# A hybrid two-layer block on one core: score steps that wait for banks, a first group by sequences, ranks by kinds of steps

## The chip, the core and the metric

The kernel runs on one core of a Trainium2 chip. The metric is device time in microseconds (us) of one execution, lower is better; of the three timed runs of the kernel before, the median is taken. Five engines work side by side: PE (matrix multiplications and transposes), DVE (vector), ACT (activations), POOL (a slower vector engine) and SP (here only issuing DMAs). Each executes its own list of instructions strictly in order; they meet through semaphores. A "bank" is one of eight 128x512 f32 accumulators that PE writes and DVE or ACT read.

## What is computed

Eight sequences of 256 tokens with 128 features pass through eight residual layers. Cut to what matters:

```python
x = x + attn_a(ln(x))       # causal attention, one head
x = x + ffn_relu(ln(x))     # 128 -> 512 -> 128, then a layernorm of its own
x = x + attn_b(ln(x))       # linear attention (no softmax)
x = x + ffn_relu(ln(x))
x = x + retention(ln(x))    # 16 heads, causal with decay
x = x + ffn_silu(ln(x))     # 128 -> 384 -> 128
x = x + softmax_attn(ln(x)) # 16 heads of 8, not causal
x = x + ffn_silu(ln(x))
```

The softmax attention is the dearest layer. For each of 8 sequences and 16 heads it needs `softmax(q k^T / sqrt(8)) v` over 256 x 256 scores, with a contraction over 8 features.

## The kernel before, in words

**Tiling.** The eight sequences form four groups (GROUPS) of two. A group's activations `x[g]` lie in the on-chip memory as 128 partitions by 4 tiles (NT) of 128 features, from the first DMA to the last. Every layer of a group starts with `normalised` (L653): bn_stats for each tile on DVE (L577), then either the aggregation on DVE (L585) with four small operations on POOL (L592 to L597), or all of it on POOL in eight small operations (L601 to L608), then scale and shift on ACT (L614) or DVE (L619), then four transposes on PE (`transposed`, L635) and a copy from the bank (`copied`, L463).

**The order of the work is planned on the host.** The layers are Python generators that yield steps: an engine (or two, `either`) with an assumed duration. The class `Plan` runs all four groups as threads against a small model of the five engines: it repeatedly takes the engine that can start soonest, and of the steps that are able to start there the one with the lowest `turn`. `turn` is the thread's rank (table RANKS by group and layer) plus a nudge for some single steps by their number (NUDGES). On PE a step that has only just become ready gets LATE added, and one that would run into the refill of instructions (256 to a page, PAGE) gets STALL times the modelled pause. `either` compares two engines with a delay for the second: SPARE for copies, SHARED for the wide two-input additions and products of `wide_step` (L468), ROOT for the retention's square root, JOINED for the aggregation of a layernorm (0.55 us: the DVE is chosen when it could begin within that of POOL's choice). The emitted programs simply follow the resulting order, so all that a change of such numbers can do is to reorder instructions, and to move some from one engine to another.

**The softmax scores.** `pairs_of_scores` (from L1155) is one thread for all sequences. A "pair" is two heads. Scores are computed twice: first with queries on the partitions, from which DVE takes the row maxima (`maxima`, L1221, two reductions a pair), then, with the maxima folded in as a ninth feature, with keys on the partitions, from which ACT makes exponentials (`exponentials`, L1255, two activations a pair). Each pair fills two banks of a pool of its own, `score_bank`, which holds four banks, and six once the last group has come to this layer (`todo["alone"]`). A contraction over 9 rows uses one of four row tiles of PE, so two pairs of opposite parity can run at the same time, in one step of 8 matmuls (L1200) instead of two steps of 4. While `alone` is false a step with two pairs always waits for four banks. When it is true, it goes with two pairs only if more than one further bank is free already, otherwise with one pair, and the other goes back into the queue. `weighted` (L1272) then multiplies exponentials by values in column tiles, L1285 transposes, L1293 and L1294 divide by the sums, L1361 transposes again, and the output projection, the last FFN and the output DMA follow.

**The first group's first layer.** `causal_attention` (L672) normalises a group, multiplies it by two prepared matrices (`value` L675 by tiles, `queries` L688 on 512 columns at once), then treats its two sequences (scores L710, mask L715, maxima L719, exponentials L722, transposes L729, values L737 to L739, and DVE's addition into `x` at L746). Group 0 arrives in two DMAs, and its layernorm is done in two halves (`halved`), but the transposes of both halves stand together in one step. `keep_busy` (L428) issues ten matmuls whose results are not used.

Of the kernel before, what the change touches and what calls it, by code (L numbers as in the profile page):

```python
# [69 lines left out]
PAGE, PAGE_US = 256, 3.7  # L70


SPARE, AIDED, ROOT, SHARED, JOINED = 0, 5.07, 0.83, 0.1, 0.55
STALL = 1.59
LEEWAY = 0


RANKS = [
    [-2.06, -5.27, -3.76, -0.29, -1.05, -0.6, -7.92, 4.73],
    [-0.06, 1.15, 4.31, 3.86, 1.11, -5.08, 0.12, 3.75],  # L80
    [1.85, 2.45, 2.73, 4.11, 1.45, 1, 1.47, 4.34],
    [3.44, 5.35, 1.93, 5.94, 3.15, 2.72, -0.21, 3.88],
]

NUDGES = {
    3: 1.5, 276: 2.4, 353: 1.8, 375: 2.8, 404: -1.8, 482: -5, 489: -3.3, 562: -1.1, 607: 2.7,
    762: 5.1, 804: 2.5, 813: -6.6, 882: 6.4, 919: -0.7, 923: 6.5, 953: 0.8, 974: 2.7, 1000: -6,
    1280: -2.1, 1282: -3.3, 1329: 8.1, 1439: 1.9, 1447: 1.8, 1560: 4, 1673: 2.9, 1798: 3.6,
}
FIRST, LAST = -15.26, 8.75  # L90
LATE = 1.25


PORT_OF_DVE = "port of DVE"
# [5 lines left out]

def of_dve(n):
    return 0.066 + n / 960


class Thread:
# [42 lines left out]
class Plan:  # L148
# [4 lines left out]
    def __init__(self):  # L153
        self.free = {e: 0.0 for e in (PE, ACT, DVE, POOL, SP)}
        self.steps = {e: [] for e in self.free}
        self.stores, self.untils, self.sleeping = [], [], []
        self.table = None
        self.mode = None
        self.port = {DVE: 0.0, POOL: 0.0}
        self.page, self.used = -PAGE_US, 77  # L160
        self.current = None
        self.count = 0
        self.made = 0
        self.now = 0.0
# [25 lines left out]
    def resume(self, th, value):  # L190
        outer, self.current = self.current, th
        try:
            want = th.steps.send(value)
        except StopIteration as stop:
            th.done, th.result = True, stop.value
            for j in th.joiners:
                self.joined(j)
            self.current = outer
            return
        self.current = outer  # L200
        self.count += 1
        kind = want[0]
        if kind == "step":
            for e, us, table, delay in want[1]:
                at = th.after(e) + delay
                self.steps[e].append((at, th, self.count, us, table))
            th.mode, th.n = want[2:]
            self.made += 1
            th.turn = th.rank + NUDGES.get(self.made, 0.0)
        elif kind == "get":  # L210
            want[1].waiting.append((th, self.count, want[2]))
        elif kind == "join":
            th.join = want[1]
            for j in want[1]:
                j.joiners.append(th)
            self.joined(th)
        elif kind == "until":
            self.untils.append((th, want[1]))
        elif kind == "at":
            self.sleeping.append((want[1], self.count, th))  # L220
# [16 lines left out]
    def stall(self, th, start, us):  # L237
# [2 lines left out]
            return 0.0  # L240
        return max(0.0, self.page + PAGE_US - start - us * (PAGE - self.used) / th.n)

    def run(self):
        self.go = []
        while True:
# [11 lines left out]
                best = (min(self.sleeping)[0], None, None)  # L257
            for e, queue in self.steps.items():
                if queue:
                    start = max(self.free[e], min(self.ready(e, q) for q in queue))  # L260
                    if best is None or start < best[0]:
                        best = (start, e, None)
            for s in self.stores:
                found = s.next()
                if found and (best is None or found[0] < best[0]):
                    best = (found[0], None, s)
            if best is None:
# [9 lines left out]
            if s is not None:  # L277
# [6 lines left out]
                self.resume(w[0], got[0] if w[2] == 1 else got)  # L284
                continue
            able = [q for q in self.steps[e] if self.ready(e, q) <= start]

            late = {id(q): e == PE and q[0] > start - LOAD for q in able}
            extra = {
                id(q): LATE * late[id(q)] + (STALL * self.stall(q[1], start, q[3]) if e == PE else 0.0)  # L290
                for q in able
            }
            q = min(
                able, key=lambda q: (q[4] not in (None, self.table), q[1].turn + extra[id(q)], q[2])
            )
            _, th, _, us, table = q
            for queue in self.steps.values():
                queue[:] = [r for r in queue if r[1] is not th]
            if table not in (None, self.table):
                us += TABLE_LOAD  # L300
                self.table = table
# [47 lines left out]
def hybrid(ctx: ExitStack, tc: tile.TileContext, t: dict, out: bass.AP):  # L349
# [290 lines left out]
        put(bank, ps)  # L640
        return yT

    def halved(a, parts):
        n = a.shape[1] // parts
        return [a[:, k * n : (k + 1) * n] for k in range(parts)]

    def normalised(g, keep=False, tiles=slice(0, NT), quick=False):
        y = yield get(work)
        nt = tiles.stop - tiles.start
        y4 = view(y, "p (t d) -> p t d", nt * D, t=nt)  # L650
        parts = 2 if quick and g == 0 else 1
        yield join(
            [  # L653
                spawn(layernorm(a, b, quick))
                for a, b in zip(halved(x[g][:, tiles, :], parts), halved(y4, parts))
            ]
        )
        yT = yield from transposed(y4, 3 if parts == 2 else 0)
        if keep:
            return y, y4, yT  # L660
        put(work, y)
# [16 lines left out]


    def causal_attention(g):  # L680
        yT = yield from normalised(g, quick=True)
        yield until(lambda: "causal" in made)
        w = made["causal"]

        def queries():
            ps = yield get(bank)
            yield step(PE, 0.86, n=4)
            nc.tensor.matmul(ps, w[:, 0, :], yT[:, :N], start=True, stop=True)  # L688
            yield from copied(q[:, :N], ps, N)
            put(bank, ps)  # L690

        def value():
            ps = yield get(bank)
            yield step(PE, 0.89)
            by_tiles(ps, w[:, 1, :], yT)
            yield from copied(values[:, :N], ps, N)
            put(bank, ps)

        def sequence(b):
            at = b * S  # L700
            v = view(values, "p (t d) -> p t d", t=NT)
            blocks = ((0, 0, P), (P, P, 3 * P))
            p = yield get(work)
            pT = yield get(work)
# [37 lines left out]
            put(work, pT)  # L742
            yield step(DVE, 0.52)
            for i in range(2):
                xs = x[g][:, 2 * b + i, :]
                nc.vector.scalar_tensor_tensor(  # L746
                    xs, ps[:, i * P : (i + 1) * P], sums[:, i : i + 1], xs, ALU.mult, ALU.add
                )
# [4 lines left out]
        values = yield get(work)  # L753
        made_v = spawn(value())
        yield join([spawn(queries()), made_v])
        yield join([spawn(sequence(b)) for b in range(2)])
        put(work, yT, q, values)

    def linear_attention(g):
# [395 lines left out]
    def pairs_of_scores():  # L1155
# [7 lines left out]
        while todo["sequences"]:  # L1163
# [22 lines left out]
            else:  # L1186
                ps = yield get(score_bank, 2)
                if len(chosen) == 2:
                    if sum(i[0] <= plan.now for i in score_bank.items) > 1:
                        ps = ps + (yield get(score_bank, 2))  # L1190
                    else:
                        of_keys, *pair = chosen.pop()
# [203 lines left out]
    plan.start(causal_weights(), FIRST, 3.8)  # L1396
    for g in range(GROUPS):
        plan.start(layers(g), g, ARRIVALS[g])
    plan.start(constants(), LAST, 29.4)
    plan.start(linear_weights(), LAST, 20.2)  # L1400
    plan.start(retention_weights(), LAST, 29.7)
    plan.start(silu_weights(), LAST, 16.5)
    plan.start(softmax_weights(), LAST, 52.5)
    plan.start(pairs_of_scores(), FIRST, 0.0)
    plan.run()
    return plan
# [103 lines left out]
```

## Time and profile before

| what | value |
|---|---|
| median of three timed runs | 427.99 us |
| the three runs | 427.99, 432.9, 426.69 us |
| the profiled execution | 426.42 us |
| its span (first to last instruction) | 424.6 us |
| mean granted PE clock in it | 0.999 |
| busy, PE / DVE / ACT / POOL | 411.2 / 311.1 / 243.1 / 180.0 us |

In the profile, a row gives the kernel's line, the engine, the operation, the tiles written and read, and the number of instructions; then busy time, the mean of one, and the idle time of the engine before them. An f32 matmul stands as two MATMUL records, a transpose as one: a score step of one pair (4 matmuls) is 8 records, one of two pairs is 16. Starts of consecutive PE records are a better measure of what a step costs than its busy time, since neighbours overlap.

By time the kernel has three parts. Until 176 us the groups work through the causal, ReLU, linear and retention layers; from 177.2 us (the first L1200) to about 352 us softmax scores are mixed with all other layers; from there to 402 us the last sequences' scores are mixed with little else, and a last stretch of 18 us finishes them.

### The profile page before, as it was taken

Reading aid. Unit: us, or ns where it says so; the run is one execution under the profiler, and the core shown is the slowest. Engines: PE = TensorE matmul, PEld = TensorE weight load, DVE = VectorE, ACT = ScalarE, POOL = GpSimd, SP = SyncE. Lnnn points to the kernel's source line nnn. Section 1 sums busy time; section 2 is a strip of 40 time slices with the busy share of each in tenths; the row PEclk is TensorE's granted clock in tenths of the full one; section 3 lists DMA queues with packets and bytes.
Section 4 is the critical chain, followed back from the end, with each engine's and each line's share of the span. In section 5 each row is a group of like instructions: output and inputs, shape, how many; then the busy total and the mean of one; then the engine's idle time right before and its main releaser. Section 6 shows DMA issues by size and latency. Waiting matters only on the chain.

```text
span 424.6 us, 12624 instructions
## 1 busy us (share of the span) xinstructions
PE 411.2 (97%) x5136; PEld 293.4 (69%) x5136; DVE 311.1 (73%) x824; ACT 243.1 (57%) x499; POOL 180.0 (42%) x358
## 2 busy tenths in 40 slices
PE   6999899999999999999999999999999999999996
PEld 6776776974777676767766657667675766665576
DVE  6997867769898969689966889833797742993253
ACT  3678867439544335424665753658645676268741
POOL 4245666575867636314696422229240300110030
PEclk9999999999999999999999999999999999999999
DMA  7400000000203001520001140000100020100001
GB/s 244 176 1 2 1 2 0 2 0 17 37 15 41 3 4 24 60 22 4 4 6 27 28 50 5 4 21 12 28 2 13 3 53 15 29 2 2 2 14 37
DMA packets 8040, 10.72 MB, mean 25 GB/s; under 512 B 1000, under 2 KB 6888, under 8 KB 7984
## 3 DMA queue, kind: packets, MB, share of 16 engines
q1 hardware_dynamic: 7904, 9.81, 11.2%
q8 instruction: 40, 0.66, 0.7%
q14 instruction: 16, 0.13, 0.2%
q10 hardware_dynamic: 80, 0.13, 0.1%
HBM read 4.43 MB, written 1.05 MB: 13 GB/s over the span
## 4 chain that ended last, share of the span: by engine, by line
PE 83%; DVE 8%; POOL 4%; ACT 2%; issue 1%; DMA 1%; POOLq 0%; DVEq 0%
PE bank L1200 18%; PE bank L1272 7%; PE bank L1130 5%; PE bank L1120 5%; PE bank L1114 5%; PE bank L819 4%; PE bank L806 4%; PE bank L1012 4%; PE bank L940 3%; PE bank L675 3%; PE bank L635 2%; PE bank L973 2%; PE bank L1285 2%; PE bank L1314 2%; DVE work L474 2%; PE bank L997 1%
## 5 line engine op out<-in xcount | busy, mean ns | idle before, releaser
L1221 DVE TENSOR_REDUCE small<-bank 128x2 f32<-128x512 f32 x128 | 80.5, 681 | 21.5 <-PE bank L1200 21.1
L1255 ACT ACTIVATE probs<-bank 128x512 f32<-128x512 f32 x128 | 67.7, 601 | 40.7 <-PE bank L1200 40.5
L1200 PE MATMUL bank<-l_spread 32*128 32x256 f32 x1024 | 85.1, 400 | 0.0
L601 POOL TENSOR_SCALAR small<-small 128x16 f32<-128x16 f32 (+1 forms) x28 | 8.0, 287 | 160.2 <-DVE small L577 160.2
L1200 PEld LDWEIGHTS bank<-l_spread 32*128 32x128 f32 x1024 | 53.6, 184 | 22.4 <-issue 7.5
L463 ACT COPY work<-bank 128x512 f32<-128x512 f32 (+3 forms) x78 | 36.7, 488 | 53.9 <-PE bank L635 21.2
L614 ACT ACTIVATE work<-x,small 128x128 f32<-128x128 f32 x84 | 36.8, 487 | 29.3 <-POOL small L608 23.9
L463 DVE COPY work<-bank 128x512 f32<-128x512 f32 (+3 forms) x34 | 17.8, 537 | 26.9 <-PE bank L1272 14.9
L577 DVE BATCH_NORM_STATS2 small<-x 128x6 f32<-128x128 f32 x128 | 29.7, 278 | 6.9 <-DMA x<-in_x 3.7
L1272 PE MATMUL bank<-probs,l_values 128*32 128x256 f32 x512 | 33.3, 384 | 0.0
L1046 POOL TENSOR_TENSOR small<-small,mhalf 128x32 f32<-128x32 f32 x6 | 32.7, 5449 | 0.5
L806 PE MATMUL bank<-work,c_relu 128*128 128x512 f32 x64 | 30.5, 599 | 1.9 <-ACT work L463 0.9
L819 PE MATMUL bank<-c_relu,work 128*128 128x128 f32 x256 | 31.0, 276 | 0.0
L819 PEld LDWEIGHTS bank<-c_relu,work 128*128 128x128 f32 x256 | 29.8, 192 | 1.2 <-issue 1.1
L607 POOL TENSOR_TENSOR small<-small,mhalf 128x4 f32<-128x4 f32 (+1 forms) x28 | 27.9, 998 | 2.2
L670 DVE TENSOR_TENSOR x<-bank,x 128x256 f32<-128x256 f32 (+1 forms) x36 | 16.1, 450 | 15.1 <-PE bank L1130 9.1
L1114 PE MATMUL bank<-work,c_ints 128*128 128x256 f32 (+1 forms) x72 | 25.1, 462 | 0.3 <-DVE work L474 0.2
L1130 PE MATMUL bank<-c_ints,work 128*128 128x128 f32 x192 | 24.5, 278 | 0.0
L1130 PEld LDWEIGHTS bank<-c_ints,work 128*128 128x128 f32 x192 | 23.2, 192 | 1.9 <-issue 1.2
L1120 PE MATMUL bank<-work,c_ints 128*128 128x256 f32 (+1 forms) x72 | 24.4, 459 | 0.0
L1272 PEld LDWEIGHTS bank<-probs,l_values 128*32 128x32 f32 x512 | 14.1, 109 | 14.0 <-issue 5.1
L635 PE MATMUL bank<-ident,work 128*128 128x128 f32 x128 | 21.3, 283 | 1.2 <-ACT work L614 1.2
(172 smaller groups left out, 781.1 us busy)
## 6 DMA issues: line engine op xcount, KB each, us to landing
r_spread<-wide SPq DMA_DIRECT2D x32, 64.0 KB
l_spread<-wide SPq DMA_DIRECT2D x32, 64.0 KB
out<-x SPq DMA_DIRECT2D x8, 128.0 KB
x<-in_x SPq DMA_DIRECT2D x3, 256.0 KB
c_retention_vo<-in_retention_vo SPq DMA_DIRECT2D x1, 713.0 KB
c_relu<-in_relu SPq DMA_DIRECT2D x1, 706.0 KB
c_retention_qk<-in_retention_qk SPq DMA_DIRECT2D x1, 641.0 KB
c_ints<-in_ints SPq DMA_DIRECT2D x1, 576.0 KB
```

Of the source, the lines that this page charges most:

```text
L463: (nc.scalar.copy if e == ACT else nc.vector.tensor_copy)(dst, src)
L614: nc.scalar.activation(y[:, i, :], src[:, i, :], AF.Identity, bias=shift[:, i : i + 1], scale=rstd[:, i : i + 1],)
L806: nc.tensor.matmul(ps, w1[:, c * P : (c + 1) * P], yT[:, :N], start=True, stop=True)
L819: nc.tensor.matmul(ps[:, n * D : (n + 1) * D], h[c][:, i * P : (i + 1) * P], w2[:, c, :], start=(c == 0), stop=(c == 3),)
L1046: nc.gpsimd.tensor_tensor(root, var, minus_half, ALU.pow)
L1114: nc.tensor.matmul(ps[:, :n], w_gate[:, cols], yT[:, :n], start=True, stop=True)
L1120: nc.tensor.matmul(ps[:, :n], w_up[:, cols], yT[:, :n], start=True, stop=True)
L1130: nc.tensor.matmul(ps[:, (i - first) * D : (i - first + 1) * D], h[c][:, i * P : (i + 1) * P], w_down[:, c, :], start=(c == 0), stop=(c == 2),
L1200: nc.tensor.matmul(to[k][:, n * S : (n + 1) * S], seq.spread[rows, j, of_keys, n * P : (n + 1) * P], seq.spread[rows, j, 1 - of_keys, :], ...
L1221: nc.vector.tensor_reduce(nmax[:, h2 % 4 // 2, 2 * (h2 % 2) + k, :], ps[k].rearrange("p (m s) -> p m s", m=2), AX.X, ALU.max, negate=True,)
L1255: nc.scalar.activation(p[:, k, :], ps[k], AF.Exp)
L1272: nc.tensor.matmul(o[32 * i : 32 * (i + 1), (j % 2) * S : (j % 2 + 1) * S], seq.v[:, c, VONE * h : VONE * h + 32], seq.p[h2][0][:, k, c * ...
```

## The change

Numbers of the plan are replaced, three pieces of code are changed, and the rest is bookkeeping that only makes the planning quicker.

```diff
-SPARE, AIDED, ROOT, SHARED, JOINED = 0, 5.07, 0.83, 0.1, 0.55
-STALL = 1.59
-LEEWAY = 0
+SPARE, AIDED, ROOT, SHARED, JOINED = 0, 5.07, 0.83, 0.1, 0
+STALL = 3.4
+WAITING = 0.6
+LEEWAY = 0.01
...
+KINDS = {
+    "add_to": -0.25, "value": 2.35, "finished": -2.57, "weighted": 0.66, "spread_heads": -0.83,
+    "pairs_of_scores": 0.61, "projected": -4.42, "down": 0.08, "maxima": -0.29, "queries": 0.54,
+    "linear_attention": 1.08,
+}
...
-FIRST, LAST = -15.26, 8.75
-LATE = 1.25
+FIRST, LAST = -7.99, 12.38
+LATE = 0.75
...
-            th.turn = th.rank + NUDGES.get(self.made, 0.0)
+            th.turn = th.rank + KINDS.get(kind_of(th.steps), 0.0) + NUDGES.get(self.made, 0.0)
...
-                    if sum(i[0] <= plan.now for i in score_bank.items) > 1:
+                    if sum(i[0] <= plan.now + WAITING for i in score_bank.items) > 1:
                         ps = ps + (yield get(score_bank, 2))
...
     def causal_attention(g):
-        yT = yield from normalised(g, quick=True)
+
+        parts = 2 if g == 0 else 1
+        n = NT // parts
+        yield join([spawn(causal_part(g, slice(k * n, (k + 1) * n))) for k in range(parts)])
+
+    def causal_part(g, tiles):
+        nt = tiles.stop - tiles.start
+        n = nt * P
+        yT = yield from normalised(
+            g, tiles=tiles, quick=True, waiting=3 if g == 0 and tiles.start == 0 else 0
+        )
...
-            yield step(PE, 0.86, n=4)
-            nc.tensor.matmul(ps, w[:, 0, :], yT[:, :N], start=True, stop=True)
-            yield from copied(q[:, :N], ps, N)
+            yield step(PE, 0.215 * nt, n=4)
+            nc.tensor.matmul(ps[:, :n], w[:, 0, :], yT[:, :n], start=True, stop=True)
+            yield from copied(q[:, :n], ps[:, :n], n)
...
-        yield join([spawn(sequence(b)) for b in range(2)])
+        yield join([spawn(sequence(b)) for b in range(nt // 2)])
```

`WAITING`: in the `alone` phase a score step with two pairs chosen takes both if two further banks come free within 0.6 us of the plan's present, and waits for them. `KINDS`: a step's turn now also depends on the generator that yields it, whatever the group. `causal_part`: group 0's first layer is two threads, one a sequence, each with its own transposes, products and copies of half the width. RANKS and NUDGES are other tables of the same form, the starting times of the five threads that prepare weights move (linear weights from 20.2 to 10.6 us of the plan, SiLU weights from 16.5 to 33.6), and JOINED becomes 0.

## The prediction

> **What bounds the kernel now.** I read the page's busy shares first, then its slices, the table of three stretches, the list of PE's waits, and last the timeline of PE where scores stand alone.
>
> ```profile
> PE 411.2 (97%) x5136; PEld 293.4 (69%) x5136; DVE 311.1 (73%) x824; ACT 243.1 (57%) x499; POOL 180.0 (42%) x358
> ...
> PE   6999899999999999999999999999999999999996
> DVE  6997867769898969689966889833797742993253
> ...
> PE 83%; DVE 8%; POOL 4%; ACT 2%; issue 1%; DMA 1%; POOLq 0%; DVEq 0%
> ```
>
> PE is busy in every slice but the first and last, and the chain that ended last lies on it for 83%. So the time is PE's own work plus what interrupts it.
>
> ```profile
> 0.00:176.00 176.00, 166.64 (x1896) 126.11 (x1897) 143.79 (x457) 102.90 (x225) 101.33 (x209) 1.00 0.15 36
> 176.00:352.00 176.00, 175.98 (x2597) 120.84 (x2595) 129.63 (x283) 100.33 (x196) 70.50 (x118) 1.00 0.12 18
> 352.00:403.00 51.00, 50.60 (x514) 31.15 (x510) 27.71 (x58) 32.35 (x63) 4.10 (x16) 1.00 0.05 10
> ```
>
> Columns: stretch, length, busy PE, PEld, DVE, ACT, POOL. PE idles 9.4 us before 176 us, where DVE is busy 82%, 0.02 us in the middle, 0.4 us in the score stretch, where DVE and ACT have room.
>
> ```profile
> PE bank L428 <- DMA x<-in_x: 3.3, 1, 3.3
> PE bank L635 <- ACT work L614: 1.2, 3, 0.5
> PE bank L806 <- ACT work L463: 0.9, 2, 0.7
> PE bank L806 <- POOL small L593: 0.9, 1, 0.9
> PE bank L710 <- DVE work L463: 0.8, 1, 0.8
> PE bank L869 <- ACT work L463: 0.7, 1, 0.7
> ```
>
> These are PE's longest waits, in total us. After the first DMA all are short: PE reaches a transpose, or a product of it, before the layernorm or the copy is through. All waits of the list but the first come to about 6.5 us.
>
> ```profile
> 351.05 1.15 PE L1200 MATMUL bank<-l_spread 32*128 32x256 f32 x16
> 352.13 0.71 PE L675 MATMUL bank<-c_softmax,work 128*128 128x128 f32 x4
> 352.77 1.13 PE L1200 MATMUL bank<-l_spread 32*128 32x256 f32 x8
> 353.83 0.44 PE L1361 MATMUL bank<-ident,work 128*128 128x128 f32 x2
> ```
>
> From start to start a score step of two pairs costs 1.08 us (351.05 to 352.13) and a step of one pair 1.06 (352.77 to 353.83): a lone pair pays nearly the price of two.
>
> **The change part by part.** The sum is made against the profiled execution: 426.42 us, span 424.6. The runs shown are 426.69, 427.99 and 432.9; the high one stands alone, so I take the mean of the two others, 427.3, as what a typical run gives, and set my result 0.9 above a profiled one.
>
> *Score steps.* In the built order of the kernel before there are 74 score steps, 54 of two pairs and 20 of one; in the changed one 71, with 57 and 14. All lone steps come behind the first 46 in both, that is in the alone stretch. So 6 x 1.06 - 3 x 1.08 = 3.1 us of PE work goes. No other engine's work changes (128 reductions of 681 ns, 128 exponentials of 601 ns stay). The Trainium skill speaks against a part of it: "TensorE: Matmul & The Clock Gate", section "Measured speedup vs the span model", gives four row tiles 3.07 times the rate of one, not 4. If two tiles gave a full 2, a step of four tiles would take 2/3.07 x 2 = 1.30 times a step of two, and the saving would be 6 x 1.06 - 3 x 1.38 = 2.2 us. The rows above show 1.02 times. I take the trace's 3.1.
>
> The price is the wait. The step of two pairs now stands in PE's order where four banks are expected up to 0.6 us late; all of PE's stream queues behind it. The banks are freed by DVE (681 ns each) or ACT (601 ns each), so a late reduction delays weighted, transposes and FFN steps alike. Bounds: nothing, if other work in front covers it (DVE 54%, ACT 63% busy there), and 0.6 us for each of the 3 new double steps, 1.8 us. Nearest row: PE's 0.4 us idle in this stretch; I take 0.4 more.
>
> *Changes of mode.* Steps between plain matmuls and the tile modes follow each other 204 times instead of 197. In the timeline a plain 128x256 matmul hands on after 0.44 us to its like (340.27 to 340.71 us), and after 0.52 us to a score step (340.71 to 341.23), so 0.08 us each: +0.6 us.
>
> *Layernorms.* JOINED at 0 sends 34 of 40 aggregations to DVE, before 12. POOL's eight rows sum to 2.72 us for four tiles (299+206+203+221+230+287+1072+199 ns), its four remaining ones to 1.78 us, and four aggregations take 0.37 us on DVE: each of 22 chains gets 0.57 us shorter. This only pays where the transposes wait. The loads for L635 were held up by L614 15 times, 5.6 us in all; at 0.37 us each, about 10 such waits cut by 0.2 to 0.57 us give 2 to 5.6. I take -2.2. POOL's share of layernorms falls by about 20 us.
>
> *Steps between engines.* DVE gains 78 aggregations (44 took 4.2 us, so +7.4), three more copies of 128x512, four of 128x256 and two of 128x384 with two fewer small ones (+4.3), four scalings (+1.4), one root (+2.5), and gives up 8 wide additions to POOL (-5.5) and three bias steps (-2.2): about +8 us, mostly before 200 us. ACT loses about 3. This is covered only while DVE is not queued: at 82% it has 32 us free there, with the 8 us 86%.
>
> *Short cover.* The moves of RANKS, KINDS and NUDGES reorder nearly everything, so I compared the two built orders at one thing that durations can price: PE steps that need a copy of an earlier PE result. For 128x512 the copy (586 ns) and two hand-overs need about 0.94 us of other PE work in between. Before, 17 places have over 0.15 us too little, 8.8 us altogether, and the trace shows them (0.84 us at L869, 1.07 us at an L806). Changed, it is 21 places and 11.4 us, several in the first layers and three after the last scores. That is +2.6 us. I have no row for the order of the rest; by this measure it is not better.
>
> *Instruction refills.* STALL doubles. Score steps of the trace that exceed their 1.08 us with no wait (1.55, 1.46, 1.39 us and the like) lose about 1.8 us together; the bounds are -1.8 and, if heavy steps now crowd elsewhere, +1.8. I take -0.9.
>
> *First group.* Its products start with the first half. In the trace the transposes start at 7.87 us behind unused matmuls from 6.00 to 7.65, and ten of those stay; what can go are waits of 0.4 and 0.9 us behind transposes up to 17 us. But four copies at half width cost fixed parts, and the two orders have like short cover there. Bounds -1.3 and +0.5; I take -0.4.
>
> No DMA is added or dropped: SP issues the same 32 + 32 spreading DMAs and the same loads. Their places move; r_spread and l_spread land while PE has other layers to do, before 352 us. Weight preparation is moved by up to 17 us, but stays in front of its first user.
>
> Sum: -3.1 + 0.4 + 0.6 - 2.2 + 2.6 - 0.9 - 0.4 = -3.0 us; 426.42 - 3.0 = 423.4 profiled, 424.3 as a typical run.
>
> **The rivals.** *Fast: the new order removes the waits as well.* If all 6.5 us of the listed waits and the 1.8 us of refills went with the 3.1 us of score steps: 426.42 - 11.4 = 415.0, or 416 typical. For it: the shorter layernorm chains act exactly where PE idles, and PE's own work does not stop it: without these waits there is nothing else in the middle. Against it: the 21 short-cover places.
>
> *Slow: DVE becomes the bound before 200 us.* The eight wide additions moved to POOL cost 1.27 us each there instead of 0.68, so POOL has 34 instead of 26. The Trainium skill, "SBUF — State Buffer", section "Summary: rules for kernel authors", says that when DVE has two inputs in that memory and POOL reads it too, the second to issue is blocked until the first is done. The trace shows such a case: a POOL operation L606 of 0.20 us took 0.77 us beside a DVE addition of 0.67. By the rows alone DVE's demand there is 144 + 8 = 152 of 176 us; by the rule in full, the 10.2 us of added POOL time block DVE too, and it is 162, 92%. From about that share on, copies queue behind aggregations, and each queue is PE's wait: if PE sees 0.3 us at each of the 37 norm transposes, +11 us, in place of my -2.2: 426.42 - 3.0 + 13.2 = 436.6, some 437.5. Against it: shorter POOL chains free 20 us of the other party.
>
> *Nothing: the merged steps only move the wait.* If DVE and ACT set the alone stretch, the 3.1 us come back as waits for banks: 427.4. PE's 50.6 busy of 51 speak against it.
>
> **How the numbers follow.** Forecast (-3 us, 420 to 429): 0.53. Nothing: 0.06. Fast, 416: 0.29. Slow, 437.5: 0.12. The time predicted is 424.3. The range 414 to 430 takes in the forecast with its bounds and most of the fast case (which has 2.5 us of spread), and leaves out the slow one and the fast end. Two per cent, 8.6 us, is about what a measurement of this kernel can tell from no change: faster means below 419.4, slower above 436.5. Faster 0.28 (nearly all of the fast case), same 0.62 (forecast, nothing, the fast and slow cases' inner ends), slower 0.10. The forecast's own range alone is 420 to 429.
>
> **What would show it.** Right: 57 score steps of 16 records at 1.08 us start to start and 14 of 8, PE still 97% busy, the alone stretch about 3 us shorter, waits of PE for L614's successor fewer and for copies more. POOL near 164 us (20 less for layernorms, 6 less for a root, 10 more for additions), DVE near 319. Wrong on the fast side: PE's waits before 176 us under 3 us altogether. Wrong on the slow side: DVE over 92% busy before 176 us, and PE waiting for DVE copies in rows over 1 us.

## The result, and the profile after

| what | before | after |
|---|---|---|
| median of 22 executions each | 428.36 us | 424.96 us |
| lowest and highest | 426.1 to 434.11 | 423.83 to 427.0 |
| profiled execution | 426.42 us | 427.0 us |

The ratio is 0.9918, 95% interval 0.9893 to 0.9942: 0.8% less, inside the 2% that counts as no change. The forecast was 424.3 us, range 414 to 430.

The two profiled executions order the kernels the wrong way round (spans 425.2 and 424.6 us): that of the changed kernel is its longest, that of before is shorter than all but one of its 22. Before's executions fall into two groups, at 425.5 to 429.1 us and, apart from single ones at 430.0 and 430.2, at 430.8 to 434.6 us, the upper one with a mean granted clock of PE of 0.988 or less, while the changed kernel has only the lower group. Where the clock stayed at 0.998 or more, before took 426.43, 426.19 and 426.12 us (medians of 11, 10 and 11 executions beside three sets of experiments below) and the changed kernel 424.80 us (21 of 22). I call these the undisturbed medians; their difference is 1.3 to 1.6 us. The clock of before's 22 executions in the table is not on record (10 of them took 430.0 us or more), so it is concluded and not measured that the rest of the 3.4 us between the two medians is the clock's.

From the page of the changed kernel, busy times and the score steps (busy us, mean ns of one, idle before):

```profile
PE 410.1 (96%) x5138; PEld 291.2 (68%) x5138; DVE 317.4 (75%) x915; ACT 239.7 (56%) x494; POOL 169.6 (40%) x275
...
L1220 PE MATMUL bank<-l_spread 32*128 32x256 f32 x1024 | 83.1, 400 | 0.0
```

DVE has 6.3 us more than before and POOL 10.4 less; the forecast named 319 and 164. L1220 is the score step (L1200 before). In PE's records it now stands as 57 groups of 16 and 14 of 8, exactly the count of the built order, and all of them from start to the next start take 78.1 us, where before they took 80.6.

The same stretches as before (busy us and number of instructions of each engine, the clock of PE behind them):

```profile
0.00:176.00 176.00, 165.81 (x1894) 125.37 (x1895) 141.00 (x495) 100.65 (x220) 109.21 (x175) 1.00 0.14 36
176.00:352.00 176.00, 175.40 (x2575) 119.03 (x2574) 138.13 (x330) 100.25 (x194) 54.29 (x80) 1.00 0.11 18
352.00:403.00 51.00, 51.00 (x545) 32.26 (x544) 28.80 (x63) 29.98 (x62) 2.67 (x8) 1.00 0.08 15
```

DVE has 141 of 176 us in the first stretch, 80%: it did not become the bound. The alone stretch is full, 51.00 of 51. The scores start at 178.7 us (177.2 before) and end at 402.6 (402.3 before): 1.2 us shorter, in the execution that is 2.2 us above its kernel's undisturbed median.

What PE waited for in this execution (us in all, times, longest):

```profile
PE bank L448 <- DMA x<-in_x: 3.5, 1, 3.5
PE bank L826 <- DVE work L483: 1.3, 2, 0.8
PE bank L839 <- DVE work L831: 1.1, 1, 1.1
PE bank L826 <- ACT work L483: 0.9, 2, 0.7
PE bank L655 <- ACT work L634: 0.9, 2, 0.5
PE bank L730 <- DVE work L483: 0.7, 1, 0.7
PE bank L1381 <- DVE work L1314: 0.5, 1, 0.5
PE bank L685 <- DVE work L483: 0.5, 1, 0.5
```

L483 is the copy from a bank (`copied`, L463 before). Of the seven rows behind the first, four are PE steps that need a copy of a PE result just made, and two more (L839, L1381) need another DVE operation on one. In no row does PE wait for a bank of scores. An estimate from PE's records, each step taken from its start to the next start and set against the shortest step of its kind in the two traces: PE's own work fell from 388.2 to 385.0 us, and what interrupts it rose from 27.8 to 30.7.

### The profile page after: what moved, and what is told of

Same layout as the page of the kernel before. It is cut to its first block, busy times and chain, and to the rows that moved or that the text cites. A ratio compares the mean times of both kernels' runs of the same rounds, so it can differ in the third digit from the quotient of the medians.

```text
span 425.2 us, 12630 instructions
## 1 busy us (share of the span) xinstructions
PE 410.1 (96%) x5138; PEld 291.2 (68%) x5138; DVE 317.4 (75%) x915; ACT 239.7 (56%) x494; POOL 169.6 (40%) x275
## 3 DMA queue, kind: packets, MB, share of 16 engines
q1 hardware_dynamic: 7904, 9.81, 10.9%
## 4 chain that ended last, share of the span: by engine, by line
PE 86%; DVE 7%; POOL 3%; ACT 2%; issue 1%; DMA 1%; DVEq 0%; POOLq 0%; ACTq 0%
PE bank L1220 18%; PE bank L1292 7%; PE bank L1150 6%; PE bank L1134 5%; PE bank L1140 5%; PE bank L839 5%; PE bank L826 4%; PE bank L1032 4%; PE bank L960 3%; PE bank L655 3%; PE bank L685 2%; PE bank L993 2%; PE bank L1091 2%; PE bank L1305 2%; PE bank L1334 2%; PE bank L889 2%
## 5 line engine op out<-in xcount | busy, mean ns | idle before, releaser
L1220 PE MATMUL bank<-l_spread 32*128 32x256 f32 x1024 | 83.1, 400 | 0.0
L1220 PEld LDWEIGHTS bank<-l_spread 32*128 32x128 f32 x1024 | 52.3, 184 | 22.3 <-issue 9.5
L483 ACT COPY work<-bank 128x512 f32<-128x512 f32 (+3 forms) x74 | 34.9, 478 | 48.1 <-PE bank L655 21.8
L612 POOL TENSOR_SCALAR small<-small 128x4 f32<-128x4 f32 (+1 forms) x34 | 9.9, 291 | 123.8 <-DVE small L605 122.8
L616 POOL TENSOR_TENSOR small<-small,mhalf 128x4 f32<-128x4 f32 (+1 forms) x39 | 38.3, 981 | 10.3 <-DVE small L613 10.3
L483 DVE COPY work<-bank 128x256 f32<-128x256 f32 (+3 forms) x41 | 21.3, 528 | 16.7 <-PE bank L1292 7.9
L839 PEld LDWEIGHTS bank<-c_relu,work 128*128 128x128 f32 x256 | 30.1, 192 | 4.3 <-issue 2.4
L839 PE MATMUL bank<-c_relu,work 128*128 128x128 f32 x256 | 31.9, 277 | 1.1 <-DVE work L831 1.1
L1066 POOL TENSOR_TENSOR small<-small,mhalf 128x32 f32<-128x32 f32 x5 | 27.7, 5536 | 0.4
L1136 ACT ACTIVATE work<-bank 128x256 f32<-128x256 f32 (+1 forms) x36 | 16.2, 454 | 18.7 <-PE bank L1134 18.3
L1150 PE MATMUL bank<-c_ints,work 128*128 128x128 f32 x192 | 25.5, 281 | 0.0
L1292 PEld LDWEIGHTS bank<-probs,l_values 128*32 128x32 f32 x512 | 13.8, 109 | 15.2 <-issue 5.1
```

The costliest lines, as they stand in the source:

```text
L483: (nc.scalar.copy if e == ACT else nc.vector.tensor_copy)(dst, src)
L616: nc.gpsimd.tensor_tensor(rstd, rstd, minus_half[:, :nt], ALU.pow)
L839: nc.tensor.matmul(ps[:, n * D : (n + 1) * D], h[c][:, i * P : (i + 1) * P], w2[:, c, :], start=(c == 0), stop=(c == 3),)
L1150: nc.tensor.matmul(ps[:, (i - first) * D : (i - first + 1) * D], h[c][:, i * P : (i + 1) * P], w_down[:, c, :], start=(c == 0), stop=(c == 2),
L1220: nc.tensor.matmul(to[k][:, n * S : (n + 1) * S], seq.spread[rows, j, of_keys, n * P : (n + 1) * P], seq.spread[rows, j, 1 - of_keys, :], ...
L1292: nc.tensor.matmul(o[32 * i : 32 * (i + 1), (j % 2) * S : (j % 2 + 1) * S], seq.v[:, c, VONE * h : VONE * h + 32], seq.p[h2][0][:, k, c * ...
```

## The experiments

Unless said otherwise, an experiment leaves the order of instructions as it is, so only its own edit differs. The four that change the condition on the banks have their own order from the alone stretch on. "Undisturbed" is as above.

### What the wait is worth

**a_wait0**: the changed kernel with the wait taken out.

```diff
-WAITING = 0.6
+WAITING = 0
```

> The changed kernel with WAITING = 0 alone. Its order is that of the changed kernel up to the alone stretch; there it has 24 lone score steps and 52 double ones in all, 76 in place of 71. Theory (PE's own work sets the stretch, a lone step costs 1.06 us): 5 x 1.06 = 5.3 us longer than the changed kernel, so about 430 us and a ratio to the kernel before of 1.004. Rival (the double steps pay their saving back as waits for banks): no longer than the changed kernel, ratio 0.992.

430.65 us (429.39 to 432.43, all 21 with a full clock), ratio to before 1.0062 (1.0036 to 1.0088). It has 76 score steps, 52 double and 24 lone, against 71: 5.85 us more than the changed kernel's undisturbed 424.80, 1.2 us for each of five steps (by the prices of a step, 10 x 1.06 - 5 x 1.08 = 5.2 us). The loss lies among the score steps: they take 230.0 us from the first to the last in the trace, in place of 224.2. So the wait is worth almost 6 us in this order, and all the rest of the change together costs: without the wait this order is 4.2 us above before's undisturbed 426.43, of which two more score steps explain 2.1.

**a_always**: the changed kernel, but a step always waits for four banks.

```diff
-                    if sum(i[0] <= plan.now + WAITING for i in score_bank.items) > 1:
+                    if True:
```

> The changed kernel where a step with two pairs always waits for four banks, as before the alone stretch: 64 steps, none alone. Theory: 7 steps less than the changed kernel, 7.4 us, less what PE waits for banks; with 0.4 us for each of 7 forced waits about 420 us, ratio 0.982. Rival: DVE and ACT cannot free the banks so fast, the waits cost as much as the steps, 425 us or more and PE waiting for L1241 and L1275 by over 5 us in all.

430.1 us (429.13 to 434.41), ratio 1.0032 (1.0001 to 1.0064). Seven steps fewer still, no lone one left, and 5 us slower. What PE waited for:

```profile
PE bank L1292 <- ACT work L1136: 1.6, 1, 1.6
```

and its end, from 352 us on (PE busy 66.10 of 77; of after's last 73.2 us it is busy 68.84):

```profile
352.00:429.00 77.00, 66.10 (x664) 43.11 (x662) 38.89 (x93) 42.37 (x81) 6.05 (x20) 0.97 0.06 15
```

PE does 2.7 us less there and idles 10.9 us instead of 4.4. The clock in this row is 0.97: it was halved for 3.4 us from 396.8 us, just behind that wait of 1.6 us, after which PE's next matmul starts at 396.4. The drop is not what costs: the one execution with a full clock took 429.34 us. Waiting pays only as far as other work covers it.

**b_wait06** and **b_always**: the two edits in the kernel before.

```diff
-                    if sum(i[0] <= plan.now for i in score_bank.items) > 1:
+                    if sum(i[0] <= plan.now + 0.6 for i in score_bank.items) > 1:
```

(in b_always `if True:`.)

> The kernel before with the 0.6 us of WAITING alone: 73 score steps in place of 74, the same order up to the alone stretch. Theory (1.06 us a step): 1 us shorter than the kernel before, ratio 0.997, and the same two groups of runs, since its first 340 us are untouched. Rival (a wait for banks eats it): ratio 1.000 or more.

> The kernel before with all double steps waiting for four banks in the alone stretch, 64 steps in place of 74. By steps alone 10.6 us shorter, ratio 0.975. After the changed kernel lost 5 us by the same (a_always, with PE idle for 6 us more from 352 us on), the theory is now that PE runs out of other work: 2 to 6 us longer, ratio 1.005 to 1.014, PE idle over 8 us from 352 us on.

b_wait06: 430.19 us (427.47 to 448.56), ratio 0.9982 (0.9933 to 1.003). Before's order gains one step of 74 by the wait, and its undisturbed median (427.66, 5 executions) is 1.5 us above before's of the same set. The upper half lies at 431 to 449: in its profiled execution the clock is halved from 123.5 us for 10.2 us, and from 376.1 for 34.1. b_always: 437.69 (434.42 to 438.72), ratio 1.0224 (1.0143 to 1.0305), with the clock halved in three places; I had expected 1.005 to 1.014. The wait brings its gain only together with the order that was made for it.

**a_split**: the changed kernel with each double step of the alone stretch issued as two lone ones, one behind the other, at the same place.

```diff
-            for n in range(2):
-                for k in range(2):
-                    for (of_keys, seq, h2), to in zip(chosen, ps):
...
+            both = list(zip(chosen, ps))
+            for part in [[b] for b in both] if todo["alone"] else [both]:
+                for n in range(2):
+                    for k in range(2):
+                        for (of_keys, seq, h2), to in part:
...
```

> The changed kernel with its plan and order untouched, but each double score step of the alone stretch issued as two lone ones one behind the other (84 groups of score matmuls in place of 71). Theory: 13 x 1.06 = 13.8 us longer, about 439 us, ratio 1.024. Rival (the stretch is set by DVE and ACT): at most half of it, since PE's extra work fits into waits, below 432 us.

425.71 us (424.58 to 428.37), ratio 0.9912 (0.9882 to 0.9942). Its undisturbed median, 425.70, is 0.9 us above the changed kernel's, where I had expected 13.8, and the two profiled executions drift apart by only 0.1 us between 345 and 420 us: next to nothing is lost. From its timeline of PE (start, us, operation, number of records):

```profile
354.48 1.16 PE L1222 MATMUL bank<-l_spread 32*128 32x256 f32 x16
355.57 0.44 PE L1383 MATMUL bank<-ident,work 128*128 128x128 f32 x2
355.94 1.13 PE L1222 MATMUL bank<-l_spread 32*128 32x256 f32 x8
357.00 0.71 PE L685 MATMUL bank<-c_softmax,work 128*128 128x128 f32 x4
```

The first line is two lone pairs in succession: 1.09 us from start to start, as a mixed double step. The third is a truly lone one: 1.06 us for half of the work. So two pairs of opposite row tiles run together whenever they are neighbours, mixed or not; a lone step is dear because a step of another kind comes next to it. What the wait buys is that they stand side by side.

### The layernorms

**b_dve_ln**: the kernel before, same order, with all 28 layernorms of POOL aggregated on DVE instead (L585's operation for each tile, then four small ones on POOL).

```diff
-            nc.gpsimd.tensor_scalar(halves, halves, -0.5, None, ALU.mult)
...
+            for i in range(nt):
+                nc.vector.bn_aggr(sums[:, i, :], flat(stats[:, i]))
```

> The kernel before, its order untouched, with all 28 layernorms of eight POOL operations aggregated on DVE and finished by four POOL operations. Theory (chains 0.57 us shorter, fewer waits of PE's transposes before 176 us): 2.2 us shorter in a quick run, and no second group of runs at 432 us, or fewer of them: median 424 to 425, ratio 0.990 to 0.995. Rival (DVE's 7 us more queue its copies): the same or longer, ratio 1.000 to 1.010.

426.96 us (425.89 to 432.8), ratio 0.9979 (0.9935 to 1.0024). The undisturbed median is 426.51 (9 executions) against before's 426.19 in the same set: no gain. The transposes of before (L635) and what held up PE and its weight loads:

```profile
L635 PE MATMUL bank<-ident,work 128*128 128x128 f32 x128 | 21.3, 283 | 1.2 <-ACT work L614 1.2
L635 PEld LDWEIGHTS bank<-ident,work 128*128 128x128 f32 x128 | 15.3, 144 | 8.3 <-ACT work L614 4.4 <-issue 2.1 <-ACT work L463 0.6
```

The same in b_dve_ln (L632):

```profile
L632 PE MATMUL bank<-ident,work 128*128 128x128 f32 x128 | 21.2, 283 | 0.9 <-ACT work L611 0.8
L632 PEld LDWEIGHTS bank<-ident,work 128*128 128x128 f32 x128 | 15.3, 143 | 7.9 <-ACT work L611 3.3 <-issue 2.3 <-ACT work L463 0.9
```

The waits for the layernorm's last step did shrink, from 5.6 us to 4.1 (0.8 + 3.3). But most of the 5.6 is idle time of the weight loads, which run beside PE's matmuls; PE itself stood still for 1.2 us before and for 0.8 here. PE is 0.7 us ahead at 113 us, level at 250, and 0.8 behind at 419. That the shorter chains give the one and DVE's longer list takes the other fits this, but is not shown. Only 2 of these 14 executions lie above 430 us, against 28 of 43 of before beside them; the edit moves the stretch of 120 us by 0.7 us, which matters below.

**a_pool_ln**: the reverse in the changed kernel, every later layernorm by POOL's eight operations.

```diff
-                for i in range(nt):
-                    nc.vector.bn_aggr(sums[:, i, :], flat(stats[:, i]))
+                by_pool()
...
```

> The changed kernel with its order untouched, but all layernorms that are not the first layer's aggregated by the eight POOL operations in place of DVE's aggregation and four POOL operations. Theory (chains get 0.57 us longer, about ten transposes wait for them): 2 us longer, up to 5.6, so 427 to 430 us, ratio 0.996 to 1.005. Rival (DVE's load is what counts, 7 us off DVE): same or shorter, 423 to 425.

443.14 us (441.06 to 445.02), ratio 1.0331 (1.0257 to 1.0406): 18 us more, three times the top of what I expected. Two stretches of 20 us hold 9 of the 16 us by which its profiled execution ends behind that of the changed kernel:

```profile
60.00:80.00 20.00, 17.02 (x97) 12.16 (x96) 12.60 (x41) 8.86 (x20) 14.36 (x36) 0.91 0.00 1
140.00:160.00 20.00, 18.37 (x256) 14.08 (x254) 16.65 (x50) 6.96 (x17) 14.22 (x22) 0.74 0.14 15
```

POOL is busy 14 of 20 us in both, PE falls to 17.0 and 18.4, and behind it the clock to 0.91 and 0.74 (halved for 3.4 us from 70.1, and for 10.2 from 141.7: 6.8 us by themselves). In the changed order the quick layernorms are not worth 2 us, they are a condition: the order counts on them.

### The clock

**b_same**: the kernel before once more.

> The kernel before once more, for its profile and its runs. In the runs beside the first four kernels it gave two groups, 20 runs from 425.9 to 429.1 us and 37 from 431.1 to 434.0, and none between; the changed kernel gave only 423.8 to 427.0. Theory (the PE clock halves for a while in some executions, where PE idles often): a profile of about 432 us shows a stretch at 0.5 of some 10 us in the first 176 us, where PE's waits are; one of about 427 us shows none. Rival (the same instructions take longer elsewhere, a DMA or an instruction refill): the clock stays at 1 and a wait of about 5 us stands in the list.

22 executions: 9 at 425.7 to 427.9 and 13 at 430.9 to 432.9, none in between; ratio 1.0021 (0.9976 to 1.0067). The profiled one has the clock halved from 53.6 us for 3.4 us and is 1.7 us later from there. Where the 430s come from it did not show; the traces of b_wait06 (the same instructions as before up to 340 us) and a_pool_ln pointed at stretches in which PE gets little done: sums over 64 rows and 17 columns, score tiles of 32 rows, or waits. I counted the multiply-adds of the records of before and took 128x512 matmuls one behind the other (0.429 us each) as dense. The poorest 3.4 us lie at 120 us, with 0.30 of dense, the next at 51 (0.33) and 204 us (0.37).

**b_fill** and **b_fill_later**: the kernel before with eight unused matmuls put into that stretch, ahead of the transposes at 121.5 us, or behind it, at 142 us.

```diff
+    calls = []
...
+        calls.append(nt)
+        if len(calls) == 17:
+            for _ in range(8):
+                nc.tensor.matmul(ps[:, :P], w1[:, :P], w1[:, :P], start=True, stop=True)
         for i in range(nt):
             nc.tensor.transpose(ps[:, i * P : (i + 1) * P], y[:, i, :], ident)
```

(18 instead of 17 in b_fill_later.)

> The kernel before with eight 128x128 matmuls (0.85 us, their result is written over by the transposes that follow) in front of the transposes at 121.5 us, in the stretch of 120 to 123.5 us where PE has the fewest multiply-adds per time of the whole run (0.31 of dense). Clock theory: about 60% of before's executions lie at 431 to 433 us because TensorE's clock is halved for about 10 us after this stretch, as in the profile of before with 0.6 in the bank condition (from 123.5 us). With the stretch filled, hardly any execution lies above 430, and the median is about 427.5 (426.7 quick, plus 0.85). Rival 1, the upper group comes from elsewhere (the chip, another stretch): the share above 430 stays near 60%, both groups 0.85 us higher. Rival 2, the fill is free because PE waits there anyway: quick executions stay at 426.7.

> The control of the run above: the same eight matmuls at the next transposes of this form, at 142.05 us, behind the stretch with few multiply-adds. Clock theory: the drop behind 123.5 us stays, about 60% of executions near 432 to 433, median about 432. Rival: any added matmuls or any shift of the later order make the upper group vanish: median 427.5 as in the run above.

b_fill: 428.46 us (427.13 to 433.08), and 1 of 22 executions above 430. b_fill_later: 433.92 us (427.67 to 434.96), 15 of 22 above 430. Before beside them: 431.43 (425.52 to 434.56), 27 of 43 above 430. The matmuls cost 1.9 us (122.53 to 124.42 in the trace), not 0.85 as expected; apart from that this is the clock theory's answer, and the control shows that it is the place that counts. Work without use in the right 3.4 us makes a typical execution 3 us shorter. The profiled execution of b_fill_later was in the upper group:

```profile
120.00:140.00 20.00, 19.39 (x334) 14.58 (x326) 13.30 (x37) 5.22 (x13) 11.14 (x10) 0.66 0.20 30
140.00:160.00 20.00, 20.00 (x338) 14.33 (x337) 17.14 (x38) 7.87 (x17) 9.22 (x21) 1.00 0.01 3
```

and around the drop (PE, start and us):

```profile
120.33 1.12 PE L1018 MATMUL bank<-r_values,work 64*64 64x17 f32 x64
121.39 0.66 PE L641 MATMUL bank<-ident,work 128*128 128x128 f32 x4
...
123.95 1.63 PE L1003 MATMUL bank<-work,wide 128*64 128x136 f32 x12
125.51 1.91 PE L1018 MATMUL bank<-r_values,work 64*64 64x17 f32 x64
```

The 64 matmuls of L1018 take 1.06 us from start to start at 120.33 and 1.84 at 125.51. The clock's record says 0.5 from 123.3 us for 13.65 us; what began at 139.0 us in the trace of before begins 6.4 us later here. In b_fill the same stretch has 1.00:

```profile
40.00:60.00 20.00, 18.29 (x95) 12.39 (x94) 15.76 (x65) 16.24 (x32) 13.42 (x27) 0.91 0.00 0
120.00:140.00 20.00, 19.72 (x423) 16.27 (x420) 16.54 (x45) 8.19 (x21) 12.53 (x12) 1.00 0.21 31
```

A small drop stays, 3.4 us from 53.3 us (the 0.91 of the first row). The Trainium skill, "TensorE: Matmul & The Clock Gate", section "What's actually happening", has the half clock after an idle window of about 3.4 us, in windows that run freely. The 3.4 us agrees: every drop here begins a whole number of 3.413 us behind the first clock record of its trace (112.64 = 33, 44.37 = 13). That the window must be idle does not: in b_wait06 PE was busy for 3.35 of the 3.41 us ahead of the drop at 123.5 us.

What goes with the drops is the count of multiply-adds, if each trace is cut into windows on this grid of 3.413 us (the last 8 us of PE's work left out). In the 14 traces, the 16 windows of full clock just ahead of a drop have 0.16 to 0.38 of dense. Of the 1624 others of full clock only one has less than 0.36 (before's at 120.0 us: 0.30, and no drop), and 15 lie between 0.36 and 0.40. Inside the drops, the 24 windows with 0.22 to 0.39 were followed by more of the half clock, the 14 with 0.44 to 0.52 by the full one. So the limit is somewhere near 0.4; this is an estimate from counts, and no run tried the limit by itself. The first clock record lies 8.6 to 11.5 us after the first instruction, and not at the same time in two executions of one kernel (10.7 us in before, 9.3 in b_same). So a poor stretch of some 3.4 us can fill a whole window in one execution and not in the next, which would make two groups of times. With the grid from 9.0 to 9.3 us (b_same, b_always, b_fill) the first drop came at 53 us; with the grid from 10.6 to 10.9 it came at 123 in b_wait06 and b_fill_later, and not at all in before.

### The short cover and the first group

**a_halfcopy**: in the changed kernel, the copy behind four transposes shared by two engines.

```diff
-        yield from copied(yT[:, : nt * P], ps[:, : nt * P], nt * P)
...
+            nc.scalar.copy(yT[:, : 2 * P], ps[:, : 2 * P])
+            nc.vector.tensor_copy(yT[:, 2 * P : N], ps[:, 2 * P :])
```

> The changed kernel, same order on PE, with the copy behind the transposes of four tiles split: ACT copies the first two tiles, DVE the other two, at the same time, instead of one engine copying all 512 columns. Theory of short cover (a PE step that needs a copy of an earlier PE result waits where less than about 0.94 us of other PE work stands between): copies of 256 columns take some 0.25 us less, so about 6 to 8 of the uncovered places lose 0.2 us each: -1 to -1.5 us, 423.5 median. Rival: the waits are for something else, or DVE's 28 added half copies (0.4 us each, 11 us) queue in front of the score and layernorm work: 0 to +3 us. If DVE were the bound before 200 us, more than that.

435.4 us (433.73 to 439.58), ratio 1.012 (1.0045 to 1.0194): some 10 us worse (undisturbed 434.35). But the edit did not do what it was written for. The view of DVE's half (durations, lowest, median and highest; what it waited for; who waited for it):

```profile
L664 DVE COPY work<-bank x27: 386/425/429, 14.3 to 352.5; 128x256 f32<-128x256 f32 x27
its engine sat idle before it (us, times) until:
  ACT work L663: 14.1, 17
who waited for it (us, times):
  PEld bank L831: 6.3, 5
  PE bank L831: 5.0, 5
...
```

DVE sat idle until ACT's half was done; in 20 of 27 places it starts 0.03 us after it. Both halves write one tile, and so the second was made to wait for the first: instead of two copies at once there is a chain of 0.37 + 0.03 + 0.41 = 0.81 us in place of ACT's single copy of 0.59, and it needs both queues in turn. At 170.8 us DVE's half stood behind a row of small operations, 1.2 us after ACT's:

```profile
170.46 0.19 DVE L881 SCALAR_TENSOR_TENSOR small<-small 128x32 f32<-128x32 f32 x1
170.68 0.19 DVE L882 SCALAR_TENSOR_TENSOR small<-small 128x32 f32<-128x32 f32 x1
170.79 0.41 DVE L664 COPY work<-bank 128x256 f32<-128x256 f32 x1
```

and PE, which had run through the changed kernel's same place without a gap, waited 1.4 us. So a shorter copy is not tried; what the run measures is a longer one: 0.22 us and a second queue at 27 places cost 9.6 us, 0.35 each. That agrees with the short cover in its sign, and says that a copy's place in its queue counts beside its length.

**b_causal**: the kernel before with the first group's attention by sequences and nothing else, planned anew.

```diff
+        parts = 2 if g == 0 else 1
+        n = NT // parts
+        yield join([spawn(causal_part(g, slice(k * n, (k + 1) * n))) for k in range(parts)])
...
```

> The kernel before with the first group's causal attention by sequences (products of 256 columns, two parts), the rest of the change left out; the indices of the order's corrections behind it are moved by the six new steps. The order is planned anew from there, so score steps are 54 double and 20 lone as before. Theory (as predicted): -0.4 us, bounds -1.3 and +0.5; up to 20 us after the start the records are at most 0.5 us earlier. Rival: the halves bring the first layer's products forward by a whole half's layernorm, 2 us or more. The new order behind it can add noise of some us either way, or move TensorE's clock drop, so that the first 30 us decide and not the total.

462.18 us (457.18 to 467.35), ratio 1.0621 (1.0497 to 1.0745). By 30 us PE has been busy 23.7 us instead of 25.7, so not even the part where the edit acts gained; and in five later places, 41 us in all, the clock is halved, which is some 20 of the 40 us by which the profiled execution (466.69 us) is longer. This does not tell what the edit is worth in the changed kernel, where PE has been busy 35.1 us by 40 us and 35.2 before. It tells that ranks and nudges fitted to one set of steps lose some 20 us on another, and the clock as much again.

## Why the prediction came out

The time was right, to 0.7 us; the sum under it only in part. The -2.2 for layernorms was far too large, the constant of +0.9 had another cause, and the two are off in opposite directions: that the time came so close is in part luck. By its own steps:

*Score steps, -3.1.* Right. The count was 57 double and 14 lone, PE's own work fell by some 3 us, and a step saved is worth 1.2 us (a_wait0). Not seen: what the wait is worth is five steps, not three, because the other edits alone would have raised the count to 76. The reason I gave, that the second pair is free in a mixed step, was too narrow: neighbours do as well (a_split).

*Banks, +0.4.* No such wait is in the trace: PE is busy 51.00 of 51 us in the alone stretch. The price is real where every step waits (a_always), not at 0.6 us.

*Layernorms, -2.2.* This step failed, and it is the term that was mis-sized. Its place was right: the waits of the transposes for the layernorm's last step fell from 5.6 us to 3.2 in the changed kernel:

```profile
L655 PE MATMUL bank<-ident,work 128*128 128x128 f32 x128 | 21.6, 283 | 0.9 <-ACT work L634 0.9
L655 PEld LDWEIGHTS bank<-ident,work 128*128 128x128 f32 x128 | 15.3, 143 | 5.8 <-ACT work L634 2.3 <-issue 1.8 <-DVE small L597 0.6
```

But "about 10 such waits cut by 0.2 to 0.57 us" was counted as time saved, and the 5.6 us were mostly waits of the weight loads. PE's own part of them went from 1.2 to 0.9 us. Done alone (b_dve_ln), the edit saves 0.7 us at 113 us and has cost 0.8 by 419. Without the term the sum is -0.8; measured undisturbed it is -1.3 to -1.6.

*Short cover, +2.6.* The direction was right. Over the whole lists of waits, PE's waits for copies from a bank rose from 3.6 us to 4.5. Those for other operations on a PE result just made, which the term did not name, rose from 0.6 to 2.6 (L839 and L1381 above). So the size fits only if both are taken together. 1.2 us of what interrupts PE in the profiled execution are chance. At 68.4 us POOL's tiny L613 met three wide operations of DVE (L488):

```profile
68.36 2.03 POOL L613 TENSOR_SCALAR small<-small 128x4 f32<-128x4 f32 x1
70.36 1.02 POOL L616 TENSOR_TENSOR small<-small,mhalf 128x4 f32<-128x4 f32 x1
68.41 1.29 DVE L488 TENSOR_TENSOR work<-work,c_relu 128x512 f32<-128x512 f32 x2
69.62 0.69 DVE L488 TENSOR_TENSOR x<-x,c_relu 128x512 f32<-128x512 f32 x1
```

In a_wait0, whose instructions are the same there, it was done at once:

```profile
68.20 0.23 POOL L613 TENSOR_SCALAR small<-small 128x4 f32<-128x4 f32 x1
68.39 1.44 POOL L616 TENSOR_TENSOR small<-small,mhalf 128x4 f32<-128x4 f32 x1
```

and PE's wait of 1.2 us for transposes at 73 us is not there. In both traces L613 starts 0.05 us ahead of the first L488. a_split has the long form (2.03 us) as well, a_always the short one. The two profiled executions with the long form are 2.0 and 2.6 us above their kernel's median, the two with the short one 0.1 and 0.6. Longer copies cost 0.35 us a place (a_halfcopy), so PE does hang on them at many places; shorter ones were not tried, and the size of the term stays unconfirmed by itself.

*Refills, -0.9.* Too large. Score steps exceed their 1.08 or 1.06 us by 2.1 us in all before and by 1.7 after (80.6 less 55 x 1.08 and 18 x 1.06; 78.1 less 57 and 14 of them; two lone steps of before stand side by side and count as one of 1.08).

*First group, -0.4; modes, +0.6.* The first was not told apart (b_causal). The second was not tried by itself. Its price stands in both traces: a 128x128, 128x256 or 128x512 matmul on the full array hands on to its like after 0.112, 0.216 and 0.429 us and to row tiles of 32 after 0.203, 0.309 and 0.523, so 0.09 us more. Such changes from the full array to smaller tiles number 73 in the records of before and 84 after, which makes about 1 us.

*From the profile to a typical run, +0.9.* This constant was probably before's lower clock in disguise. Beside the experiments, executions of before with a mean clock of 0.995 or 0.996, which is what one drop of 3.4 us makes, took 427.2 to 429.1 us, and of the three runs shown (426.69, 427.99 and 432.9) the second lies among them and the third in the upper group. I took the spread for noise. Undisturbed the kernel is at 424.80, not 423.4, and 21 of its 22 executions have no clock drop to be added.

*The rivals.* Fast fell with the waits: they are not gone, they changed places. Slow fell with DVE at 80% before 176 us, below the 86% I had reckoned; the 18 us of a_pool_ln show that a POOL or DVE queue can cost as much as that case said. "Nothing" fell with the full alone stretch.

So the gain is 1.3 to 1.6 us where the clock is full: about 6 us by the wait, given back for the most part by an order that needs more of it. Some 2 us more in the median come from the clock. In before it falls for some 7 us or more in 59 to 65% of the executions beside the experiments, in the changed order in none. That the drop at 123 us is what makes before's upper group is shown by b_fill and its control. Why the changed order is spared is only argued: on the clock's own grid its poorest window in the profiled execution has 0.41 of dense, and that of a_wait0, with no drop in 21 executions, 0.36. None of the twelve experiments beat the changed kernel.

## What to carry to other kernels

Where a kernel's times fall into two groups, look at the granted clock of each execution: here one stretch of 3.4 us made the difference, and a few matmuls without use in the right 3.4 us can be worth more than a tuned step. Judge a wait that brings equal small-tile steps together by what stands next to them, and by the other work that covers it. A shorter chain in front of a busy engine is worth what the end gains, not what the wait lost; and where an order was fitted to a set of steps, testing one edit in the old order and undoing it in the new one gives two different answers (no gain and a loss of 18 us here).

## What the hardware showed

PE's clock is halved for whole windows of 3.413 us (3.4, 6.8, 10.2, 13.7, 17.1 and 34.1 us were seen), and that behind windows in which PE does less than about 0.4 of dense work, be it waiting (busy 0.47 of the window before the drop at 141.7 us in a_pool_ln) or busy with small tiles (0.98 in b_wait06). It costs about half the stretch: 1.7 us for the shortest, 6.4 for one of 13.65. Two groups of matmuls on different row tiles overlap across a step's border: 1.09 us for both, 1.06 for one alone. Behind a 128x256 matmul on the full array, its like starts after 0.216 us and a row tile of 32 after 0.309. A POOL operation on 128x4 took 2.03 us beside DVE's two-input operations in two executions and 0.23 in two others with equal instructions and equal starts.
